# A conditioned attention block with two transformer layers: the first sequences loaded in rows, the layers' weights loaded behind the first projections, local scores in units of two heads, and a new order

## The chip, the core and the metric

The kernel runs on one core of a Trainium2 chip. Its engines work side by side: TensorE (PE) multiplies matrices and transposes, VectorE (DVE), ScalarE (ACT) and GpSimd (POOL) do the element-wise work, and SyncE (SP) as well as ScalarE issue DMAs. The metric is the device time of one execution in microseconds. All arithmetic is in 32-bit floating point.

## The reference, cut to what matters

There are 32 independent sequences of 256 tokens with 256 features. A sequence `x` and a side sequence `f` go through one conditioned attention (16 heads of 16) and two layers of local attention (8 heads of 64, windows of 128 tokens, each with the window before it) with a gated feed-forward part (hidden width 682); the result is added to `x`.

```python
# conditioned attention, for each sequence
q = (f + b_self) @ Wq + bq
k_prev, k_self = (x + b_prev) @ Wk + bk, (f + b_self) @ Wk + bk
v_prev, v_self = x @ Wv + bv, f @ Wv + bv
weights = softmax([masked(q k_prev^T), q . k_self] / 4)
h = (weights[:-1] @ v_prev + weights[-1] * v_self) @ Wo + bo
# two layers
for l in range(2):
    q, k, v = split(shift_token(h) @ wqkv[l])
    q, k = rotary(l2norm(q) * q_scale[l]), rotary(l2norm(k) * k_scale[l])
    h = h + local_attention(q, k, v) @ wo[l]
    n = layernorm(shift_token(h)) * ln_g[l] + ln_b[l]
    a, g = split(n @ w1[l] + b1[l])
    h = h + (a * gelu(g)) @ w2[l] + b2[l]
return x + h
```

## The kernel before

The kernel takes sequences in pairs (`G = 2`), so there are sixteen pairs. For each of the two sequences of a pair it runs `prepared` (load, turn, project) and `conditioned` (scores, softmax, values, output projection). Then come, for the pair, two rounds of `attention` for each sequence and `feedforward` for both together. `finished` loads `x` once more, adds, and stores. The features lie on the partitions between these steps, in one of two `stream` tensors.

None of this is issued in the order in which it is written. Every operation is first recorded in a `Plan` as part of a unit, the work that TensorE does without a break, with what the other engines do on its results. A unit has a kind: `full` uses the whole array, `rows` of 2 or 4 and `cols` of 2 or 4 divide it into tiles that work side by side. A full unit with 128 output rows that follows a `cols` unit may be run in column halves or quarters. The planner (`Plan.run`) then goes through a model of the engines and picks at each moment the ready unit with the lowest score (`policy`, line 1399). The score grows with the unit's place in the program (`AGE` times `stand`, where `stand` takes a table of shifts, `SHIFT`, with `FIRST` for the first pair and `FINAL` for the last two), with a change of tiling (`SWITCH`), with the work that the unit would heap on another engine beyond `STAY` (same tiling) or `ENTER` (new tiling), and falls with the work that it feeds (`FEED`, at most `MOST`). The other engines take what has been ready longest (`rank`, line 538). The order found is then issued from one line, so all instructions of the profile have line 567, and they are told apart by the names of their tiles. PSUM has eight banks, and SBUF tiles come from four pools (`t2`, `t4`, `e6`, `sm`); a unit starts when its tiles are free.

What the change touches:

- `load_sequence` (line 697) loads `ft` (of `f`) and `xt` (of `x`) through `blocks`, four DMAs of 64 KB each with runs of 128 bytes, on SP's queue. In this layout DVE can turn a whole tensor with one 32x32 block transpose. `prepared` (line 874) does so into `fT` and `xT`. For the first two sequences the loads are recorded before the loop.
- `prepared` projects `fT` and `xT` with `wq`, `wk` and `wv`. The tiles of the results are `cq`, `ck`, `cs` and `vals`. ScalarE adds the biases into `qc` and `kc`, and `spread` sends these with eight small SP DMAs each into `qh` and `kh`, where each head has its own partitions; `kh<-behind` adds a mask row. The unit `self` is its last.
- `conditioned` makes scores twice: `S` for the maximum (`mx`), and, once the maximum is written into `qh` (`nmT`, `rows`), `ST` for the exponentials `eT`, which `AV` weighs. `co` is the output projection.
- The weights are loaded from ScalarE's queue. `wq`, `wk`, `wv`, small vectors and constants (`misc`, whose first columns are the identity `ident`) come first, then `wo` and `bo`, and then a loop over the two layers (line 781) with `wqkv`, the rope table (`rope0`, scaled by `qks`), `wout`, `w1`, the small vectors and `w2`. Nothing holds these loads back.
- `attention` (line 1042) handles a sequence's eight heads as four pairs `c`. `scores(cs)` (line 1107) makes the scores `sc` of the pairs in `cs` in one unit of kind `rows` 2 and hands them to `weights`, which makes `ex` with DVE and ScalarE. `turned` transposes these (`exT`) and `weighed` multiplies by `v` (`av`). How many pairs make one unit is set by `CS, CX, CW = 2, 2, 2`, for the three steps in turn.

Of the kernel before, what the change touches and what calls it, by code (L numbers as in the profile page):

```python
# [19 lines left out]
P = 128  # L20
S = 256
D = 256
G = 2
# [134 lines left out]
class Plan:  # L158
# [15 lines left out]
    def __init__(self, tc, engines, pools, make):  # L174
        self.tc, self.engines, self.pools, self.make = tc, engines, pools, make
        self.nodes, self.units, self.unit_, self.group, self.place = [], [], None, 0, 0.0
        self.stage, self.stages, self.done = 0, {}, set()
# [116 lines left out]
    def run(self, policy):  # L294
# [18 lines left out]
        self.idle = self.switches = self.cold = self.wire = 0.0  # L313

# [42 lines left out]
        while todo:  # L357
# [12 lines left out]
            if e != "PE":  # L370
# [12 lines left out]
                if n.load:  # L383
                    self.wire = max(self.wire, end) + n.load
                    end = self.wire + self.LANDING
                ended(n, end)
# [151 lines left out]
    def rank(self, n, e):  # L538
        other = e == "S" and n.table not in ("any", None, self.table)
        return n.ready + 2.0 * other, n.number  # L540
# [32 lines left out]
class Engine:  # L573
# [11 lines left out]
CS, CX, CW = 2, 2, 2  # L585
# [3 lines left out]
    156, 528, 54, -76, 49, 292, -28, 245, 120, -102, -425, 52, -30, 35, 68, 22, 33, 22, -208,  # L589
    -4, 119, -41, 61, 69, 90, 152, 19, 32, -62, -238, 52, -2, 49, -168, 13, -85, -54, -65, 36,  # L590
    64, 112, -439, -349, -167, 223, -408, -5, 62, -46, -234, 56, -27, 119, -7, -45, 96, -17,
    -38, 61, -374, -335, -58, 1, -150, -372, -152, -51, -265, -409, 8, 67, -53, 114, -41, -17,
    -83, 34, 68, 48, 60, -261, -99, -7, -76, -335, -100, -105, -191, -306, -58, 15, -102, 32,
    -23, -66, 39, -309, -188, 106, -258, 33, -30, -139, 22, -141, 82, -290, -255, 32, 19, -99,
    134, 126, 14, -15, -222, -574, -156, 97, 93, -32, -241, 50, 152, -118, -41, -45, 21, -102,
    20, 47, 3, 15, 55, 169, -56, -24, 43, 199, -247, 143, -97, -15, -223, -41, -95, -88, -212,
    -127, -29, -32, -285, -545, -142, -265, -8, -118, -6, 152, 84, -122, 25, 14, 4, 18, 141, 60,
    166, -454, -139, 25, -127, -186, -20,
]
FIRST = [  # L600
    0, 0, 0, 0, 0, 0, 0, 0, 10, 35, -9, 213, 102, 95, 210, -345, -65, -122, -290, 49, -201, 6,
    -193, -61, -7, 106, 99, -6, -100, -16, 106, 13, 65, -266, -137, 7, -58, 247, 58, 69, 48, 1,
    -114, -155, -32, -173, -34, 65, 135, 130, -117, 69, 71, 117, 272, 156, 73, -3, -1, -31, -33,
    -133, 51, 151, 175, 239, 445, 215, 231, 120, 135, 97, -3, -90, -188, -357, -32, -64, -276,
    -297, -374, -330, -535, -346, -72, -135, -217, 156, 27, 182, 40, -174, -48, 77, -252, -118,
    -307, -246, 33, -96, -400, -238, -150, -69, -239, 6, 79, 152, 26, -38, -60, -358, -15, -155,
    89, -99, -69, -60, 87, -3, -114, -222, -118, 60, -143, -246, -29, -171, -319, -115, -49,
    -17, -96, -75, -88, 113, 144, -56, -6, 35, -9, -141, -41, -74, -183, -115, -131, -49, -79,
    109, -65, -145, 55, -88, -244, -157, -153, -264, -181, -118, -121, -82, -23, -37, -86, -83,
    -110, -213, -219, -209, -160, -63, 0, 0,  # L610
]
FINAL = [
    0, 0, 0, 0, 0, 0, 0, 0, 56, -34, 24, 16, 12, 140, -55, -63, -14, 1, -33, -84, -66, -53, -46,
    -145, -40, -121, 67, -19, -32, -29, 98, 97, 8, 45, -119, -130, -61, -106, 67, 94, -33, 8,
    54, 33, 8, -94, -222, -47, -210, -95, -90, -11, -121, 156, 49, 10, 43, 87, 7, 64, -144, -81,
    35, -80, 47, -31, -76, -182, 53, 86, 32, 67, 229, 49, 115, 31, 6, -10, -135, 40, 27, -79,
    -83, -8, 108, -110, 63, -40, -249, -98, -95, -18, -170, -139, -28, -12, -41, 76, 83, 116,
    59, -9, 65, -157, -74, -50, -119, -145, -16, -25, 13, 6, 73, -2, -181, -184, -151, -49, -97,
    116, -8, 56, 187, 15, 69, -31, -42, -59, 109, 161, 193, 112, 209, 211, 117, 80, 41, 59, 77,
    -84, 136, 47, 92, -54, 145, 66, 93, 1, -60, 152, -30, 108, 108, -119, 50, -9, -29, -39, 44,  # L620
    -113, -118, -128, -103, 66, 10, -89, -27, -49, -2, -10, 53, 34, -67, -8,
# [4 lines left out]
def tile_kernel(ctx: ExitStack, tc: tile.TileContext, a: dict, out: bass.AP):  # L626
# [69 lines left out]

    def load_sequence(n, after=()):
        plan.unit(after=after)
        loaded[n] = [blocks(name, src[n]) for name, src in (("ft", f), ("xt", x))]

    load_sequence(0)
    plan.unit()

# [5 lines left out]
    wq, wk, wv = (weight(f"w{n}", a[f"L0_cond_W{n}"], D) for n in "qkv")  # L709
# [10 lines left out]
    bk = column(a["L0_cond_bk"], "bk", 2)  # L720
    bv = kept("bv", (P, D))
    ld(bv, a["L0_cond_bv"].partition_broadcast(P), act)
    ld(misc, a["c_misc"][:, 0:C_IOTA], act)
# [45 lines left out]
    load_sequence(1)  # L769
# [3 lines left out]
    plan.unit()  # L773
    wo = weight("wo", a["L0_cond_Wo"], D)
    bo = column(a["L0_cond_bo"], "bo", 2)
    rope0 = sb2("rope0", P, 2, 4, FD)
    ld(rope0, a["c_rope"].rearrange("(t p) j d -> p t j d", p=P), act)
# [3 lines left out]
    for l in range(DEPTH):  # L781
# [63 lines left out]

    def projected(name, w, j, src):
# [605 lines left out]
```

## Time and profile before

| what | us |
|---|---|
| median of 3 runs (3422.1 to 3424.76) | 3423.85 |
| the profiled execution | 3422.27 |
| its span, first to last instruction | 3420.5 |
| TensorE busy | 3348.6 |
| VectorE busy | 2161.9 |
| ScalarE busy | 1780.5 |
| GpSimd busy | 1163.4 |

The profile is of one execution. A row of a timeline gives the start, the duration, the engine (with a q for the issue of a DMA), the line, the operation, the output and inputs by name, the number of instructions merged into the row, and, in brackets, the idle time before it with what ended it. A row of the stretches gives the stretch, its length, the busy time and instructions of PE, PEld (weight loads), DVE, ACT and POOL, then the granted TensorE clock as a share of full speed, the busy share of the DMA engines, and GB/s.

### The profile page before, as it was taken

The numbers are of one execution on the slowest core, as the hardware profiler recorded it, in microseconds if no ns is written. First come the engines' busy times: TensorE is split into PE (matmuls) and PEld (weight loads), VectorE is DVE, ScalarE is ACT, GpSimd is POOL, SyncE is SP. The second block draws the span as 40 slices with busy tenths as digits, with TensorE's granted clock in tenths as the row PEclk, the third lists the DMA queues.
The fourth block names the chain that finished last, engine by engine and source line by source line (L and its number), as shares of the span: only waits on it lengthen the run. The fifth ranks groups of instructions, "written<-read, shape, count | busy, mean of one in ns | idle before, by whom it ended". The sixth has DMA issues, their size and how long they took to land.

```text
span 3420.5 us, 69279 instructions
## 1 busy us (share of the span) xinstructions
PE 3348.6 (98%) x25984; PEld 1908.7 (56%) x25984; DVE 2161.9 (63%) x6673; ACT 1780.5 (52%) x4537; POOL 1163.4 (34%) x1195
## 2 busy tenths in 40 slices
PE   6999999999999999999999999999999999999998
PEld 5665556465564655656455564655646556465554
DVE  3558567485675747657485674847657486574763
ACT  0556456473554726456373563735547364554653
POOL 0325052250613407043160522507134070432541
PEclk7999999999999999999999999999999999999999
DMA  5100010010101001010010100101010010100001
GB/s 147 20 15 11 12 27 9 16 26 9 26 15 21 17 13 20 16 20 17 13 21 14 27 13 15 24 7 26 16 20 17 13 20 15 27 15 12 4 2 27
DMA packets 310926, 69.00 MB, mean 20 GB/s; under 512 B 286776, under 2 KB 308096, under 8 KB 310592
## 3 DMA queue, kind: packets, MB, share of 16 engines
q1 hardware_dynamic: 298848, 54.24, 9.3%
q10 hardware_dynamic: 11744, 10.34, 1.1%
q8 instruction: 207, 3.39, 0.4%
q14 instruction: 127, 1.04, 0.1%
HBM read 35.53 MB, written 8.39 MB: 13 GB/s over the span
## 4 chain that ended last, share of the span: by engine, by line
PE 77%; DVE 12%; POOL 3%; ACT 1%; issue 1%; POOLq 0%; SPq 0%; DMA 0%; DVEq 0%; ACTq 0%
PE w L567 27%; DVE ex L567 6%; PE wout L567 6%; PE q L567 5%; PE av L567 4%; PE k L567 4%; PE sc L567 4%; PE S L567 4%; PE v L567 3%; PE ST L567 3%; PE vals L567 3%; PE AV L567 3%; PE exT L567 2%; PE qkT L567 2%; DVE rot L567 2%; PE cs L567 2%
## 5 line engine op out<-in xcount | busy, mean ns | idle before, releaser
L567 ACT ACTIVATE ex<-ex,nm,rq 128x128 f32<-128x128 f32 (+1 forms) x1024 | 546.2, 537 | 107.3 <-DVE nm L567 106.1
L567 PE MATMUL w<-cen,w 128*128 128x512 f32 (+2 forms) x1480 | 589.2, 598 | 0.8 <-DVE cen L567 0.3
L567 POOL TENSOR_TENSOR raw<-raw,rot 128x512 f32<-128x512 f32 x256 | 327.6, 1281 | 749.2 <-DVE rot L567 660.3
L567 PEld LDWEIGHTS w<-cen,w 128*128 128x128 f32 (+2 forms) x1480 | 224.9, 175 | 270.7 <-issue 231.4
L567 DVE TENSOR_SCALAR ex<-ex,den 128x128 f32<-128x128 f32 (+1 forms) x1024 | 351.4, 457 | 5.2
L567 DVE TENSOR_REDUCE mx<-S 128x2 f32<-128x512 f32 x512 | 314.3, 686 | 49.4 <-PE S L567 49.3
L567 PE MATMUL w<-act,w 128*128 128x512 f32 (+3 forms) x880 | 324.6, 602 | 2.9 <-DVE act L567 2.8
L567 ACT ACTIVATE eT<-ST 128x512 f32<-128x512 f32 x512 | 263.8, 605 | 115.0 <-PE ST L567 109.8
L567 DVE CUSTOM_DVE_ANT_0 ex<-sc,misc 128x128 f32<-128x128 f32 (+1 forms) x1024 | 299.2, 353 | 31.3 <-PE sc L567 30.8
L567 DVE SCALAR_TENSOR_TENSOR act<-w,b,act 128x512 f32<-128x512 f32 (+1 forms) x192 | 143.4, 748 | 262.0 <-PE w L567 195.5
L567 ACT ACTIVATE act<-w,b 128x512 f32<-128x512 f32 (+1 forms) x192 | 128.9, 686 | 280.1 <-PE w L567 276.8
L567 POOL TENSOR_TENSOR xs<-stream 128x512 f32<-128x512 f32 x32 | 35.0, 1094 | 641.5 <-PE cs L567 318.1
L567 PE MATMUL wout<-qT,wout 128*64 128x256 f32 (+2 forms) x1728 | 242.8, 381 | 0.5 <-DVE nm L567 0.3
L567 PE MATMUL v<-wqkv,stream 128*128 128x512 f32 (+1 forms) x608 | 242.5, 599 | 0.0
L567 PE MATMUL k<-wqkv,stream 128*32 128x512 f32 (+2 forms) x1104 | 239.9, 593 | 0.0
L567 PE MATMUL q<-wqkv,stream 128*32 128x512 f32 (+2 forms) x960 | 237.7, 594 | 0.2 <-ACT stream L567 0.2
L567 ACT COPY exT<-exT 128x384 f32<-128x384 f32 x512 | 207.3, 498 | 54.5 <-PE exT L567 53.8
L567 PEld LDWEIGHTS w<-act,w 128*128 128x128 f32 (+3 forms) x880 | 124.8, 176 | 167.1 <-issue 151.5
L567 POOL TENSOR_TENSOR rq<-ss,minus_half 128x8 f32<-128x8 f32 x128 | 215.1, 1684 | 4.9
L567 POOL TENSOR_TENSOR ss<-ss,minus_half 128x8 f32<-128x8 f32 x128 | 213.3, 1666 | 5.7
L567 PE MATMUL sc<-kT,qT 64*128 64x128 f32 (+1 forms) x2048 | 205.7, 337 | 0.4
L567 PEld LDWEIGHTS wout<-qT,wout 128*64 128x64 f32 (+2 forms) x1728 | 161.6, 147 | 73.0 <-issue 17.6
(127 smaller groups left out, 5520.2 us busy)
## 6 DMA issues: line engine op xcount, KB each, us to landing
ft<-in_fside_BxSxS_dram SPq DMA_DIRECT2D x128, 64.0 KB
xt<-in_x_dram SPq DMA_DIRECT2D x128, 64.0 KB
qh<-qc SPq DMA_DIRECT2D x256, 32.0 KB
kh<-kc SPq DMA_DIRECT2D x256, 32.0 KB
ot<-in_x_dram SPq DMA_DIRECT2D x128, 64.0 KB
out_dram<-ot SPq DMA_DIRECT2D x128, 64.0 KB
wqkv<-in_L_ffn_wqkv_dram ACTq DMA_DIRECT2D x2, 1536.0 KB
w<-in_L_ffn_w_dram ACTq DMA_DIRECT2D x2, 1364.0 KB
```

The source lines that it names most:

```text
L567: ins = getattr(self.engines[n.engine], name)(*[real(v) for v in args], **{k: real(v) for k, v in kw.items()})
```

## The change

The diff has five parts, and what they compute stays the same.

1. The first two sequences are loaded by `rows`: one DMA for each tensor, token rows of 1 KB. `prepared` turns these with `turned_tiles`, which is four TensorE transposes into a PSUM bank and a copy by DVE or ScalarE. Later sequences keep `blocks`. The identity is loaded ahead of all weights, and the loads of sequence 1 are recorded before those of the lengths.
2. The loop over the layers becomes `load_layer(l, after)`. It is called in the loop over the pairs, in the first pair, after `prepared` of sequence 0 for layer 0 and of sequence 1 for layer 1, and its unit waits for the last unit of that `prepared`. The unscaled rope table is loaded once for each layer. `wv` follows the small vectors, and `wo` and `bo` have a unit of their own.
3. `CS` becomes 1, so that `scores` makes a unit for each pair of heads.
4. The planner's model of a DMA issue now waits until the eighth transfer back has landed, and `rank` can weigh the place in the program by `hurry`, which is set to 0.
5. The constants of the score and the three tables of shifts are new.

```diff
     def put(n):
...
                 if n.load:
-                    self.wire = max(self.wire, end) + n.load
+
+                    at = max(t, self.landed[-8]) + cost
+                    now[e] = at
+                    self.wire = max(self.wire, at) + n.load
                     end = self.wire + self.LANDING
+                    self.landed.append(end)
...
-        return n.ready + 2.0 * other, n.number
+        return n.ready + 2.0 * other + self.hurry * n.unit.stand, n.number
...
-CS, CX, CW = 2, 2, 2
+CS, CX, CW = 1, 2, 2
...
+    def rows(name, src):
+
+        t = sb2(name, P, 2, D)
+        ld(t, src.rearrange("(t p) d -> p t d", p=P))
+        return t
...
     def load_sequence(n, after=()):
         plan.unit(after=after)
-        loaded[n] = [blocks(name, src[n]) for name, src in (("ft", f), ("xt", x))]
+        shape = rows if n < G else blocks
+        loaded[n] = [shape(name, src[n]) for name, src in (("ft", f), ("xt", x))]

     load_sequence(0)
     plan.unit()
+    ld(ident, a["c_misc"][:, C_ID : C_ID + P], act)
...
-    wq, wk, wv = (weight(f"w{n}", a[f"L0_cond_W{n}"], D) for n in "qkv")
+    wq, wk = (weight(f"w{n}", a[f"L0_cond_W{n}"], D) for n in "qk")
...
+    wv = weight("wv", a["L0_cond_Wv"], D)
     bv = kept("bv", (P, D))
     ld(bv, a["L0_cond_bv"].partition_broadcast(P), act)
-    ld(misc, a["c_misc"][:, 0:C_IOTA], act)
+    ld(misc[:, P:C_IOTA], a["c_misc"][:, P:C_IOTA], act)
+    load_sequence(1)
+    plan.unit()
...
-    for l in range(DEPTH):
+
+    def load_layer(l, after):
+        plan.unit(after=after)
+        rope0 = sb2("rope0", P, 2, 4, FD)
+        ld(rope0, a["c_rope"].rearrange("(t p) j d -> p t j d", p=P), act)
         wqkv.append(weight(f"wqkv{l}", a["L0_ffn_wqkv"][l], 3 * INNER))
...
         ft, xt = loaded.pop(n)
-        plan.unit()
-        fT, xT = sb2("fT", P, 2, S), sb2("xT", P, 2, S)
-        for dst, src in ((fT, ft), (xT, xt)):
-            vec.transpose(dst.rearrange("p c t -> p (c t)"), flat(src))
+        if n < G:
+            fT, xT = turned_tiles("fT", ft), turned_tiles("xT", xt)
+            plan.unit()
+        else:
+            plan.unit()
+            fT, xT = sb2("fT", P, 2, S), sb2("xT", P, 2, S)
+            for dst, src in ((fT, ft), (xT, xt)):
+                vec.transpose(dst.rearrange("p c t -> p (c t)"), flat(src))
...
             heads.append(prepared(n, b))
+            if p == 0:
+                plan.stage = (-1, 1 + b)
+                load_layer(b, (plan.unit_,))
...
-    STRETCH, AHEAD, LAST = 2.75, 3, 14
-    AGE, SWITCH, OVER, STAY, ENTER = 0.02, 1.5, 1.0, 6.0, 4.0
+    STRETCH, AHEAD, LAST = 2.5, 3, 14
+    AGE, SWITCH, OVER, STAY, ENTER = 0.02, 0.5, 0.5, 8.0, 1.5
     HURRY = 0.0
-    FEED, MOST, BANKS = 1.0, 3.0, 0.0
+    FEED, MOST, BANKS = 1.0, 2.0, 0.5
```

## The prediction

> **What bounds the kernel now.** I read four views in this order: the page's busy rows and slices, the table of stretches, the timeline of the first 120 us, and TensorE's waits and timeline in one period of the middle. From the page:
>
> ```profile
> span 3420.5 us, 69279 instructions
> PE 3348.6 (98%) x25984; PEld 1908.7 (56%) x25984; DVE 2161.9 (63%) x6673; ACT 1780.5 (52%) x4537; POOL 1163.4 (34%) x1195
> ...
> PE   6999999999999999999999999999999999999998
> ...
> PEclk7999999999999999999999999999999999999999
> ```
>
> TensorE is busy in 98% of the span; no other engine reaches two thirds. So time can come only from TensorE: its idle time (71.9 us), its slow clock, or its own work. The first slice is the odd one: 6 tenths busy, clock 7. The stretches (PE busy, then the other engines, the granted clock, DMA share and rate) open it up:
>
> ```profile
> 0.00:10.00 10.00, 2.21 (x11) 2.24 (x11) 2.09 (x7) 0.00 (x0) 0.50 (x5) 1.00 0.79 156
> 10.00:20.00 10.00, 3.04 (x15) 2.95 (x14) 0.49 (x5) 0.00 (x0) 1.89 (x1) 1.00 1.00 249
> ...
> 40.00:50.00 10.00, 6.06 (x29) 5.97 (x28) 0.27 (x2) 0.00 (x0) 0.00 (x0) 0.50 0.77 230
> 50.00:60.00 10.00, 6.48 (x32) 4.67 (x32) 3.83 (x12) 0.00 (x0) 0.45 (x2) 0.50 0.42 93
> ...
> 80.00:90.00 10.00, 10.00 (x65) 6.83 (x58) 5.64 (x10) 1.96 (x5) 0.00 (x0) 0.50 0.01 3
> ```
>
> Over all stretches to 120 us, idle is 28.6 us. Busy time multiplied by the missing share of the clock gives another 22.9 us, and the first query projections (3.78 us, where the same eight records take 1.99 us at 65.69) 1.9 us that the clock column misses. So about 53 us are lost before 120 us. From 120 to 3400 us the same table has 31.8 us of idle at clock 1.00, and the last 20.5 us have 11.5. Why the opening is slow is in its timeline:
>
> ```profile
> 17.03 4.81 SPq L567 DMA_DIRECT2D ft<-in_fside_BxSxS_dram  x4
> ...
> 22.09 3.78 PE L567 MATMUL cq<-fT,wq 128*128 128x256 f32 x8 [9.05 <-DVE fT L567]
> ...
> 32.41 1.28 ACT L567 ACT_TABLE_LOAD   x1 [32.41 <-DMA w<-in_L_ffn_w_dram]
> ...
> 33.70 0.47 ACT L567 ACTIVATE qc<-cq,bias_q 128x256 f32<-128x256 f32 x1
> ...
> 50.60 4.55 PE L567 MATMUL S<-kh,qh 17*128 17x256 f32 x22 [4.54 <-DMA w<-in_L_ffn_w_dram]
> ...
> 62.20 0.47 ACT L567 ACTIVATE kc<-ck,bias_kp 128x256 f32<-128x256 f32 x1 [26.93 <-PE ck L567]
> ```
>
> Three delays stand in a row. First, the sequence's loads (eight DMAs of 128-byte runs) and a length load queued behind them hold fT until about 22 us. Second, `cq` is done at 25.9, yet `qc` starts at 33.70, because ScalarE's stream holds the layer-0 DMA issues ahead of it. Third, layer 1's issues (33.71 to 58.4) do the same to `kc` of sequence 1. Each queue pauses as if about eight transfers may be open: ACT's ninth issue waits at 6.94, SP's ninth at 12.47, when earlier ones land.
>
> **The change, part by part.**
>
> **Sequences 0 and 1 in rows.** Sixteen SP issues become four, with 1 KB runs instead of 128 bytes; four DVE transposes (0.69 us each) become sixteen TensorE transposes and four copies (0.69 us on DVE or 0.58 on ScalarE). Sequence 1 also no longer waits in SP's queue at 17.03. Before cq, about 1.1 MB must arrive (ft, xt, identity, wq, wk): 7 us at the 156 GB/s of the first stretch, 3 us at the 371 GB/s of 20 to 25 us, plus issue and landing. I take fT at 8.5 us (7 to 12), so cq some 13 us earlier. In the trace, four turns of `at` take 0.60 us warm. The Trainium skill, "TensorE: Matmul & The Clock Gate", Part 4, speaks against this move: a transpose isn't counted as activity and doesn't release the clock. The sum by the warm row is 4 × 0.60 = 2.4 us, by the rule 4.8 us with all of them cold. The first two sets surely run cold, so I take 3.6 us. They stand on the path, since nothing else is ready.
>
> **Layers loaded behind projections.** The ACT queue first gets identity, wq, wk, four small vectors, wv, bv, the masks, wo and bo; a layer's sixteen issues come only after the last unit of a sequence's `prepared`. So `qc` and `kc` of sequence 0 have nothing of the layers ahead: `qc` at about 14 us instead of 33.7, spreads (20 small SP DMAs, which took 35.2 to 58.7 us beside the weights) mostly ahead of or beside layer 0. I put the first S stage at 30 us where it ended at 60. What is late next is the same ScalarE block in another place. The sixteen issues of layer 0 ran from 9.1 to 33.3 and those of layer 1 from 33.7 to 58.4, 24 us each; after the change I expect some 20 to 40 and 42 to 62. Queued behind them are sequence 1's `qc` and `kc`, then the first `eT`; S, self and AV on TensorE wait for these. The first ST stage therefore moves from 85.88 to about 60, and the first q projection from 115.28 to about 88. The rope table, now read twice, adds 256 KB, about 1 us of DMA that weights cover. Opening in sum, transposes included: **-28 us**, bounds -12 and -40 (the whole 53 us cannot go: 8 us of arrival and a cold start stay).
>
> **One score unit for two heads.** The matmuls, mask additions and exponentials stay; 128 score units of sixteen records become 256 of eight. Each asks two banks instead of four. TensorE's price is in these rows (start, duration):
>
> ```profile
> 1102.49 3.19 PE L567 MATMUL sc<-kT,qT 64*128 64x128 f32 x32
> 1105.62 1.07 PE L567 MATMUL AV<-eT,vh 128*32 128x256 f32 x16
> ...
> 1157.61 1.58 PE L567 MATMUL sc<-kT,qT 64*128 64x128 f32 x16
> 1159.02 0.91 PE L567 MATMUL exT<-misc,ex 64*128 64x64 f32 x24
> ...
> 1179.25 1.58 PE L567 MATMUL sc<-kT,qT 64*128 64x128 f32 x16
> 1180.76 1.99 PE L567 MATMUL wout<-qT,wout 128*128 128x256 f32 x8
> ```
>
> From start to next start a unit takes 1.41 us when another row-tiled unit follows and 1.51 when a full one does: one change of tiling costs about 0.10 us. An added unit costs 0 where it stands beside row-tiled work and 0.20 alone: 0 to 26 us over 128 units. The skill's "TensorEngine Tiling (Array Packing)", Key Properties, says that changing mode drains the engine; read strictly, every added unit pays twice, 26 us, and the opening's gain is gone. The trace says that much score and transpose work adjoins. I take 0.07, **+9 us**. Against it, DVE is fed 4 us at a time (four mask passes, 2 × 0.29 + 2 × 0.42, reads, four scalings of 0.40 to 0.52) instead of 8, and fewer banks are held; TensorE's small waits on DVE and ScalarE after 120 us sum to about 28 us. I take a third of these, **-10 us**; bounds -20 and 0.
>
> **Order found anew.** The price lists of the planner change: a switch of tiling counts 0.5 instead of 1.5, backlog is tolerated to 8 instead of 6 when staying and to 1.5 instead of 4 when entering. This reshuffles everything with the same work. From 1000 to 1210 us I count 60 changes of tiling; at 0.10 us and sixteen pairs this is about 96 us of span. A cheaper switch invites more, a stricter entry fewer. Bounds -24 and +24 (a quarter either way); I take **0**. The end (PE from 3401.81, DVE, POOL, output DMA) has no edit of its own: 0, bounds -3 and +3.
>
> Sum against the profiled execution, 3422.27 us (3420.5 of span and 1.8 around it): 3422.3 - 28 + 9 - 10 = 3393. The median shown, 3423.85, is 1.6 above that execution, so I forecast **3395 us**.
>
> **The rivals.** *Weights and spreads collide* (0.20): layer 0 starts just as sequence 0's spreads do, and those need 20 us again as at 35 to 58. For it: DMA runs at 178 to 322 GB/s there; against: fewer bytes are left. The opening gives 12 and the middle stays: 3422.3 - 12 - 1 + 1.6 = 3411. *Tiling switches eat it* (0.14): smaller units and a switch price of a third raise changes from 60 to 90 per pair; 480 × 0.10 = 48 us on TensorE itself (the added score units are among these changes), against 28 won in the opening, with the middle's waits unchanged: 3422.3 + 48 - 28 + 1.6 = 3444. It decides from about 280 added changes, 17 per pair. For it: TensorE has no slack to hide them; against: neighbours of equal tiling cost nothing. *The two halves balance* (0.06): 3424. That the layers don't move at all is excluded only if the planner heeds the new edge; nothing it prices may bring them ahead of that unit.
>
> **How the numbers follow.** The main case has 0.60. A measurement of this kernel can tell about 0.2%, 6.8 us, from no change. Main and collision cases give faster 0.80; balance gives 0.06, switching 0.14. The range reaches from an opening of -40 and a middle of -16 (3368) to most of the switching case (3430), leaving about 0.2 out.
>
> **What would show it.** Right: PE's first slice at 8 or 9; `cq` before 10 us; `qc` before 17 without a wait for a layer's DMA; first q projection at 80 to 95; idle to 120 us under 18. PE busy after 120 us within 15 us of 3257. Wrong: S still waiting on kh spreads beyond 45 us (collision), or `sc` and the changes of tiling adding over 28 us of TensorE time after 120 (switching).

## The result, and the profile after

The kernel after takes **3460.64 us** (3458.92 to 3462.82), beside 3423.47 for the kernel before in the same comparison: a ratio of 1.0109, interval 1.0091 to 1.0126. It is 37 us slower, where 29 us less was forecast. The page of the kernel after (busy rows, TensorE's slices and clock, then the shares of the chain that ended last):

```profile
span 3457.1 us, 67916 instructions
PE 3373.3 (98%) x25400; PEld 1965.6 (57%) x25400; DVE 2184.5 (63%) x6737; ACT 1764.7 (51%) x4473; POOL 1174.6 (34%) x1195
...
PE   7999999999999999999999999999999999999998
...
PEclk7899999999999999999999999999999999999999
...
PE 63%; DVE 20%; ACT 6%; POOL 5%; issue 2%; DMA 0%; SPq 0%; POOLq 0%; DVEq 0%; ACTq 0%
```

The same chain in the kernel before:

```profile
PE 77%; DVE 12%; POOL 3%; ACT 1%; issue 1%; POOLq 0%; SPq 0%; DMA 0%; DVEq 0%; ACTq 0%
```

The shares of busy time tell nothing: TensorE is at 98% in both. The chain does. Work that leads to the end passes through DVE, ScalarE and GpSimd for 31% of the span, against 16% before.

Where the time went is seen from one marker, the first reduction `mx<-S` on DVE of each pair of sequences (the sixteen pairs are counted from 0, and the order repeats from pair to pair). Three stretches, in us; the marker stands at another place in the new order, so only the period and the total compare exactly:

| kernel | start to pair 5 | pair 5 to pair 15 | pair 15 to end | one period (mean of six) |
|---|---|---|---|---|
| before | 993.1 | 2025.1 | 402.3 | 207.3 |
| after | 993.3 | 2055.2 | 408.6 | 210.15 |
| difference | +0.2 | +30.1 | +6.3 | +2.85 |

So the gain that was forecast for the opening does not show (the first stretch also holds pairs 0 to 4; the sums to 120 us below are of the opening alone), and most of the loss is made in the repeating part: nearly 3 us in every pair.

**The opening.** TensorE's stretches (columns as before):

```profile
0.00:10.00 10.00, 4.91 (x21) 3.93 (x22) 2.88 (x6) 0.00 (x0) 0.19 (x4) 1.00 0.78 200
10.00:20.00 10.00, 10.00 (x38) 8.98 (x39) 0.87 (x7) 2.28 (x4) 2.39 (x3) 1.00 0.20 54
...
40.00:50.00 10.00, 3.33 (x16) 3.37 (x16) 1.89 (x9) 0.00 (x0) 0.45 (x2) 0.50 0.72 227
50.00:60.00 10.00, 6.84 (x31) 6.59 (x31) 0.27 (x2) 0.00 (x0) 0.00 (x0) 0.50 0.75 224
...
80.00:90.00 10.00, 10.00 (x69) 8.73 (x70) 3.89 (x9) 0.37 (x1) 0.00 (x0) 0.50 0.01 2
```

The first 20 us are much better than before, and DMA, at 100% then, now runs at 54 GB/s. The bytes come later, at 40 to 60 us, and there the hole is. To 120 us TensorE idles 24.4 us instead of 28.6, but the half clock now takes 27 us of its busy time instead of 23 (the last row above: TensorE full, at 0.50): the two cancel. The clock column has no record before 18 us, where a set of turns takes 1.1 us instead of 0.60. The timeline of TensorE and ScalarE:

```profile
4.33 1.09 PE L572 MATMUL turn<-misc,ft 128*128 128x128 f32 x4 [4.33 <-DMA ft<-in_fside_BxSxS_dram]
...
14.11 2.05 PE L572 MATMUL cq<-fT,wq 128*128 128x256 f32 x4
...
16.20 0.47 ACT L572 ACTIVATE qc<-cq,bias_q 128x256 f32<-128x256 f32 x1 [0.39 <-PE cq L572]
...
46.66 8.66 PE L572 MATMUL b<-lb,w 128*128 128x1 f32 x40 [11.15 <-DMA lb<-in_L_ffn_ln_b_dram]
...
59.34 3.81 PE L572 MATMUL S<-kh,qh 17*128 17x256 f32 x16 [3.16 <-DMA kh<-kc]
...
68.41 0.47 ACT L572 ACTIVATE kc<-ck,bias_kp 128x256 f32<-128x256 f32 x1 [40.22 <-DMA lb<-in_L_ffn_ln_b_dram]
```

and of SP's queue:

```profile
24.77 13.89 SPq L572 DMA_DIRECT2D qh<-qc  x16
38.76 13.48 SPq L572 DMA_DIRECT2D kh<-behind  x8
52.34 22.86 SPq L572 DMA_DIRECT2D kh<-kc  x16
```

`cq` starts 8 us earlier and `qc` 17.5 us earlier than before, and then all is given back: the new order issues the spreads of both sequences' `qh` first, then eight `behind` rows, and only then `kh`. The spread that the first S stage needs last is the 32nd issue; before it was the 20th. S starts at 59.34 (before 50.60). The last `kc` stands behind the layers' issues for 40 us, and the first q projection comes at 117.78 instead of 115.28.

**The score units.** The `sc` group on the page (busy, mean ns, idle before it and its releaser), after and before:

```profile
L572 PE MATMUL sc<-kT,qT 64*128 64x128 f32 (+1 forms) x2048 | 207.7, 337 | 9.0 <-ACT kT L572 5.8
```

```profile
L567 PE MATMUL sc<-kT,qT 64*128 64x128 f32 (+1 forms) x2048 | 205.7, 337 | 0.4
```

Twice the units cost 2 us of work in the new order, in which a score unit follows another at 141 places; changes of tiling, counted by the shapes of TensorE's records, fell from 1011 to 965 in the whole program. What grew is the wait in front of them.

**One period.** TensorE's waits from marker to marker, kernel after (us in total, times, longest):

```profile
PE ck L572 <- DVE xT L572: 1.2, 1, 1.2
PE sc L572 <- ACT kT L572: 0.5, 1, 0.5
PE cq L572 <- DVE fT L572: 0.4, 1, 0.4
PE qkT L572 <- POOL raw L572: 0.4, 1, 0.4
PE self L572 <- DVE prod L572: 0.3, 1, 0.3
```

and before:

```profile
PE exT L567 <- ACT sq L567: 0.5, 1, 0.5
PE turn L567 <- POOL at L567: 0.2, 1, 0.2
PE qkT L567 <- DVE rot L567: 0.2, 1, 0.2
```

From start to start of TensorE's records, a pair has 205.9 us of work and 1.4 of waits before, 207.1 and 3.0 after. The longest of these waits is for `xT` on DVE, which stands at the end of a stretch in which DVE has no gap:

```profile
1133.00:1153.00 20.00, 19.63 (x93) 11.19 (x92) 20.00 (x60) 14.56 (x46) 15.96 (x16) 1.00 0.17 27
1153.00:1173.00 20.00, 18.69 (x154) 11.58 (x155) 14.55 (x39) 11.88 (x31) 14.94 (x15) 1.00 0.11 23
```

DVE is busy 20.00 of 20 us (in fact for 40.2 us, from 1125.1 to 1165.3; the longest such run in a period of before is 20.5 us), and TensorE's worst row follows.

### The profile page after: what moved, and what is told of

It reads as the page before. It is cut to its first block, busy times and chain, and to the rows that moved or that the text cites. A ratio compares the mean times of both kernels' runs of the same rounds, so it can differ in the third digit from the quotient of the medians.

```text
span 3457.1 us, 67916 instructions
## 1 busy us (share of the span) xinstructions
PE 3373.3 (98%) x25400; PEld 1965.6 (57%) x25400; DVE 2184.5 (63%) x6737; ACT 1764.7 (51%) x4473; POOL 1174.6 (34%) x1195
## 4 chain that ended last, share of the span: by engine, by line
PE 63%; DVE 20%; ACT 6%; POOL 5%; issue 2%; DMA 0%; SPq 0%; POOLq 0%; DVEq 0%; ACTq 0%
PE w L572 27%; DVE ex L572 9%; PE wout L572 5%; PE S L572 4%; ACT ex L572 4%; PE av L572 4%; PE ST L572 3%; POOL raw L572 3%; PE AV L572 2%; PE vals L572 2%; PE k L572 2%; PE v L572 2%; PE q L572 2%; PE exT L572 2%; DVE rot L572 2%; DVE raw L572 2%
## 5 line engine op out<-in xcount | busy, mean ns | idle before, releaser
L572 PE MATMUL w<-act,w 128*128 128x512 f32 (+2 forms) x780 | 326.2, 605 | 0.0
L572 PEld LDWEIGHTS w<-act,w 128*128 128x128 f32 (+2 forms) x780 | 127.0, 187 | 165.0 <-issue 158.7
```

Source lines behind the costliest of these rows:

```text
L572: ins = getattr(self.engines[n.engine], name)(*[real(v) for v in args], **{k: real(v) for k, v in kw.items()})
```

## Experiments

In all of them the planner's list of units is kept as it is in the kernel named, and then edited by a function `moved(order)`; no order is found anew. `earlier(order, preds, n, stop)` moves a unit or instruction up to the first place that its inputs and its buffers allow. Each ratio is to the kernel before, which took 3424.4 to 3425.8 us in these comparisons.

One thing has to be taken out before the periods of these runs are compared. In six periods of before and of after (pairs 5 to 10) the clock is granted in full. In after_dve, after_halves, after_full, after_ex_halves and after_best some periods hold a stretch of 3.41 us (in after_full up to 6.83) at half clock. Two neighbouring periods of after_dve and two of after_best:

```profile
995.90:1206.10 210.20, 206.81 (x1570) 120.82 (x1569) 137.05 (x421) 109.49 (x279) 73.14 (x74) 1.00 0.10 18
1206.10:1417.90 211.80, 208.36 (x1570) 121.91 (x1569) 137.20 (x422) 109.57 (x279) 73.18 (x74) 0.99 0.10 17
```

```profile
1195.40:1402.50 207.10, 205.14 (x1900) 105.13 (x1898) 133.61 (x414) 113.03 (x287) 73.14 (x74) 1.00 0.10 18
1402.50:1611.10 208.60, 206.62 (x1900) 105.82 (x1898) 133.67 (x413) 112.85 (x287) 73.23 (x74) 0.99 0.10 18
```

The same instructions take TensorE 1.5 us longer. What brings the clock down in one period and not in the next, no run shows; in after_dve it falls within 1 us after a wait of 2.1 us, in after_best some 2 us after one of 0.6. "Undisturbed" below means a period without such a stretch.

### The opening: queues

**after_pool**: the layers' loads on GpSimd's queue.

```diff
+    loads = [n for n in order if n.engine == "S" and n.load and n.unit.stage in ((-1, 1), (-1, 2))]
+    kept = [n for n in loads if not n.tiles]
...
+    for n in kept:
...
+        n.engine = "G"
+        stop = earlier(order, preds, n, stop) + 1
```

> The kernel after, its order kept, but the layers' weights (except the rope table and the q and k scales) are issued from GpSimd's queue right after the first loads, so that they move while the DMA engines stand at 0 to 69 GB/s (15 to 30 us) and ScalarE has nothing to hold it from 27.8 to 68.4 us. Theory 'the delayed loads eat the opening's gain': kc of sequence 1 at about 28 us instead of 68.4, the first q projection before 100 us instead of 117.8, the kernel 15 to 22 us faster than the kernel after. Rival 'weights and spreads collide whatever the queue': the spreads of qh and kh still end after 60 us, gain under 6 us.

Measured 3455.59 us, 1.0092 (1.0075 to 1.0110): 5 us better than after. The loads now start at 1.3 us and compete with what is needed first: `cq` moves from 14.1 to 21.6, and the `kh` spreads still end at 63, as the rival said.

**after_pool2** and **before_pool2**: only the twelve large loads go there (in the kernel after behind GpSimd's copy into `kh`, so from 14 us).

```diff
+    big = sorted((n for n in order if is_weight(n)), key=lambda n: n.number)
...
+    stop = copied[0] + 1
+    for n in big:
...
+        n.engine = "G"
+        stop = earlier(order, preds, n, stop) + 1
```

> The kernel after, its order kept, but the twelve large weight loads are issued from GpSimd's queue after its copy into kh (about 13 us), layer 0 first, the small ones stay on ScalarE's. The first try (all loads from GpSimd at 1 us) put cq back from 14.1 to 21.6 us and won 5 us. Theory 'the delayed loads eat the opening's gain': cq stays at 14 us, the weights move from 13 to 45 us, kc of sequence 1 is done at 32, first q projection at 95 to 105 us instead of 117.8, 12 to 20 us faster than the kernel after. Rival 'the spreads collide with the transfers in any order': under 6 us.

> The kernel before, its order kept, but the twelve large weight loads of the layers are issued from GpSimd's queue after its copy into kh (about 12 us) instead of ScalarE's. Theory 'the opening is held by ScalarE's blocked queue': qc starts at 24 us instead of 33.7 and kc of sequence 1 is not held to 62; the first q projection comes 10 to 20 us sooner, about 3410 us, faster than both kernels. Rival 'the spreads and the transfers set it': the kh spreads still end near 58 us, within 5 us of the kernel before.

after_pool2: 3456.32 us, 1.0091 (1.0076 to 1.0106). SP's spreads in it:

```profile
24.87 25.88 SPq L572 DMA_DIRECT2D qh<-qc  x16
```

The same sixteen spreads took 13.89 us above; beside 330 to 386 GB/s of weights they take 25.88, and S starts at 58.65. before_pool2: 3439.43 us, 1.0043 (1.0028 to 1.0058). There the loads went out at 1.3 us, and the eight loads of the first sequence in 128-byte runs were issued on SP only by 35.8 us (in before by 12.4):

```profile
40.81 3.78 PE L567 MATMUL cq<-fT,wq 128*128 128x256 f32 x8 [16.45 <-DVE fT L567]
```

Another queue takes a load out of a sequencer's way, not out of the way of other transfers. The Trainium skill, "DMA: Bandwidth & Descriptors", Issuing engines are not separate DMA queues, says so too, and adds that concurrent issue saves only sequencer time; the two rows bear it out and put a price on it.

**after_kc**: all `qc` and `kc` and all spreads ahead of the layers' issues, the first S unit with them, the `b1` units behind the first q projection. **before_kc**: each layer's loads behind `kc` of its sequence, `b1` late.

```diff
+    for n in early:
+        if order.index(n) > stop:
+            stop = max(stop, earlier(order, preds, n, stop) + 1)
+    return bias_late(order)
```

> The order of after is kept, with three things moved in the opening: all qc and kc evictions and all qh/kh spreads of both sequences go ahead of the 32 layer loads in ScalarE's and SP's streams, the first S unit goes up with them, and the two b1 units go behind the first q projection on TensorE. If what ate the opening's gain is that spreads run beside the weights and that kc of sequence 1 and b stand behind the layers' issues: first S at about 45 us instead of 59, first q projection at 100 to 106 instead of 118, and 10 to 16 us off the time, 3445 to 3451. If the opening's loss is the cold clock and the amount of work, and the waits only fill it: first q within 3 us of 118 and the time within 4 us of 3460. The period of 210 us per pair stays in both.

> The order of before is kept, with the same idea: each layer's 16 loads stand behind kc of its sequence in ScalarE's stream, and the two b1 units go behind the first projections; sequences are still loaded in blocks and score units are whole. If the blocks of layer issues ahead of qc and kc are what makes before's opening slow: qc starts at about 26 instead of 33.7, S at 45 to 50 instead of 50.6 to 60, first q projection at 101 to 107 instead of 115, and 8 to 14 us off 3425: 3411 to 3417, which would beat both kernels. If weights behind the projections only move the collision, as the comparison of the two traces says for after: within 4 us of 3425. The period of 207.2 us stays in both.

Both theories missed: 3475.50 us, 1.0150 (1.0135 to 1.0165) and 3449.64 us, 1.0072 (1.0057 to 1.0087), 15 and 25 us slower than their parents. Nearly all of it is in the first stretch (1008.3 and 1014.4 us), the period is the parents'. In after_kc the S stage starts at 53.56, no more than 6 us earlier: even with every `kc` done by 32 us the 32nd of SP's issues sets it. The first q projection comes at 114.41 instead of 117.78. The loss stands behind it: the `b1` units, which ran at half clock in idle time, now stand in the path from 119.03 to 134.97 (5.1 and 1.0 us for one layer, 8.7 and 1.0 for the other), at half clock from 123.0 on. In before_kc S does start at 40.89 instead of 50.60, but then `cq` of sequence 1 waits 9.76 us for `mx` on DVE, the first q projection comes at 114.90 (before 115.28), and `b1` fills 126.47 to 144.30. So these two runs mix two moves: the place of the loads was worth 3.4 and 0.4 us to the first q projection, and the place of `b1` cost 16 to 18. No run moved the loads and left `b1`.

**after_spq**: SP's spreads in the order of need (sequence 0 first), layer 0's loads behind `kc`, layer 1's weights on SP behind the rows, each `b1` later.

```diff
+    spreads.sort(key=lambda n: (n.unit.stage, "b" not in name_in(n), n.number))
...
+    order = behind(order, preds, set(loads[0] + small), last)
+    order = behind(order, preds, set(weights), rows)
+    for n in weights:
+        n.engine = "D"
```

> The order of after is kept, but the opening's queues are put in the order in which they are needed: SP spreads sequence 0 first (behind, qh, kh), then sequence 1; the layer loads stand behind kc of both sequences in ScalarE's stream, with the weights of layer 1 moved to SP behind the rows of both sequences; each layer's b1 unit stands where a bank comes free later. Theory (spreads): S waited until 59 because its last spread was the 32nd of 40 issues on SP, at 0.9 to 1.7 us each. Eight qc spreads from 25 us and eight kh spreads at 0.62 each put the first S at 36 to 40, the first q projection at 95 to 108, and the time at 3440 to 3452. Rival (the knot): with S early, the next in-order queue (DVE's rope products that wait for a layer's loads, or ScalarE's issues) takes the wait and b1 loses its idle time: first S early, but first q within 6 us of 118 and the time at 3456 or more.

The rival was right: 3473.87 us, 1.0148 (1.0131 to 1.0165). S starts 13 us earlier than in after, the first q projection comes no earlier (118.08, after 117.78), and the start to pair 5 takes 7 us longer; some 5 of these are `b1` of layer 1, which now runs behind that projection, from 135.47. TensorE, DVE and GpSimd in it:

```profile
45.99 8.54 PE L572 MATMUL S<-kh,qh 17*128 17x256 f32 x50 [10.93 <-DMA kh<-kc]
63.51 3.26 PE L572 MATMUL S<-kh,qh 17*128 17x256 f32 x14 [8.98 <-DVE mx L572]
```

```profile
62.09 0.77 DVE L572 TENSOR_TENSOR rope<-rope,qks 128x64 f32<-128x64 f32 x6 [7.66 <-DMA qks<-in_L_ffn_k_scale_dram]
```

```profile
109.02 0.45 POOL L572 COPY w1t<-w 128x84 f32<-128x84 f32 x2 [21.98 <-DMA lg<-in_L_ffn_ln_g_dram]
...
110.69 1.48 PE L572 MATMUL turn<-misc,at 128*128 128x128 f32 x4 [10.62 <-POOL at L572]
```

`mx` is ready to run but stands behind a rope product that waits for a layer's scales; `at` stands behind GpSimd's copy that waits for layer 1's weights. With SP's order mended, DVE's and GpSimd's in-order streams hold TensorE instead. So the order of the spreads did delay S, but S alone was not what the opening was short of: SP has 32 issues up to the one that S needs, and ScalarE's, DVE's and GpSimd's in-order streams each have something that waits for a layer's DMA ahead of a sequence's work.

### Score units and column halves

**before_split**: each score unit of before in two, the second half behind the next unit on TensorE (1011 changes of tiling become 1047).

```diff
+            held = Node("PE", None, n.number)
+            held.ops, held.soft, held.tiling, held.parent = n.ops[4:], False, n.tiling, n
+            n.ops = n.ops[:4]
```

> The kernel before, its order kept, but each score unit of two pairs of heads is cut into two and the second half is issued after the next unit of TensorE (where no reader forbids it). This adds 36 changes of tiling (1011 to 1047 in the whole program). Theory 'a half unit costs little': 36 changes at 0.10 us and somewhat later masks, 2 to 10 us slower than the kernel before. Rival 'every unit pays its own drain' (the switching case of the prediction): 128 times 0.20, 26 us slower or more, which would explain most of the loss.

3437.76 us, 1.0041 (1.0027 to 1.0054): 12 us, 1.0 us in each period: +0.57 per pair as waits of `ck` on DVE, +0.45 as TensorE's own time. That is about the size that the prediction gave the split by itself, but it had counted changes of tiling alone.

**before_full** and **after_full**: nothing in column halves or quarters.

```diff
+        if n.engine == "PE" and n.soft and n.ops:
+            n.tiling = ("full", 1)
```

> The kernel before, its order kept, but no full unit is run in column halves or quarters any more. Before, 700 us of TensorE's time went in column halves after 120 us, in the kernel after 411 us. Theory 'the new order loses the column halves': they save time on the narrow outputs (var, self) and on the weight loads of v, k and q; without any the kernel before is 15 to 30 us slower, and the kernel after has lost some 40% of that. Rival 'halves cost and save nothing': within 5 us of the kernel before.

> The kernel after, its order kept, without any column halves or quarters. Leaving them out of the kernel before cost it 37 us (3462.6 against 3425.5). Theory 'the new order uses the halves less': after 120 us the kernel after spends 411 us in halves where the kernel before spends 697 us, so leaving them out costs about 37 x 411 / 697 = 22 us, 3483 us, and some 15 us of the change's loss is this. Rival 'both orders gain the same by halves': 37 us again, 3498 us, and the halves explain nothing of the loss.

3462.56 us, 1.0115 (1.0097 to 1.0134), and 3491.71 us, 1.0199 (1.0165 to 1.0232): 37 us for before. For after the size is unclear: its four executions spread from 3480.82 us at a mean clock of 0.989 to 3508.23 at 0.982. The first is 20 us over after, which had 0.989 too. Undisturbed periods say the same: 211.8 us in after_full, 1.6 more than after, where before_full has 3.2 more than before. So the halves are worth about 1% to before and some 0.6% to the new order, near the 22 us of the first theory. They pay at the matmuls with 1 or 8 output columns: var +0.84 and self +0.80 us per pair in before_full. The new order has fewer: 411 us of TensorE's time in halves after 120 us, where before has 697.

**after_halves** and **before_halves**: the opposite, each unit that can run in halves does.

```diff
+        if n.engine == "PE" and n.soft and n.ops and n.tiling == ("full", 1):
+            n.tiling = ("cols", 2)
```

> The order of after is kept, but every matmul unit that could run in column halves and runs whole in after does run in halves (TensorE time in column halves after 120 us is 411 us in after, 697 in before). If the column halves that the new order has lost are worth their time (var and self with outputs of 1 and 8 columns cost 0.84 and 0.80 us per pair more when before runs them whole): var and self fall by at least 0.9 us per pair and the time by 10 to 20 us, 3440 to 3450. If halves only pay where a neighbour is in halves already, since each further change of tiling costs about 0.1 us, or because twice the instructions cost as much: within 5 us of 3460 or slower.

> The order of before is kept, and every soft matmul unit that ran whole in it runs in column halves. Before waits only 1.4 us per pair and its period is TensorE's own work, so if each half of a small matmul saves what the ledger says (0.37 us per pair for var and 0.37 for self in after), it could fall by up to 6 us, to 3418, and beat both kernels; but before has most of these in halves already (697 us of 3257), and added changes of tiling at transposes (0.1 us each, exT and vals +0.4 and +0.5 per pair in after) may cost as much: within 5 us of 3425.

3449.71 us, 1.0070 (1.0053 to 1.0086), and 3423.18 us, 0.9998 (0.9989 to 1.0008). In after, 11 us come back, but not where expected: the profile has -5.0 us before pair 5, -2.3 at the end, and none in between. There two things eat the gain. In an undisturbed period (209.3 us, 0.8 less than after) TensorE's work is 1.3 us less (var and self -0.37 each; `exT` +0.4) and its waits are 0.56 us more. And most periods hold a stretch at half clock, which gives 1.5 us back, at `vals` and `rs`. That 0.56 of 1.3 us comes back as waits says that TensorE alone does not set the period any more. In before nothing is won: changes of tiling rise from 1011 to 1163, TensorE's work rises by 0.7 us per pair and its waits fall by 0.5.

### What sets the period

**after_dve**: the transposes into `fT` and `xT`, for which `cq` and `ck` wait, up to eight DVE instructions earlier. **after_act**: the copies `oh`, `aT` and `av` from DVE to ScalarE.

```diff
+        while i > 0 and k < EARLY:
+            i -= 1
+            k += order[i].engine == "V"
+        earlier(order, preds, n, i)
```

```diff
+        if n.engine == "V" and hasattr(n, "either") and n.ops[0][1][0].tile.name in ("oh", "aT"):
+            n.engine = "S"
+        elif n.engine == "V" and hasattr(n, "either") and n.ops[0][1][1].tile.name == "av":
+            n.engine = "S"
```

> The kernel after, its order kept, but each transposition of fT and xT stands eight VectorE instructions earlier in VectorE's stream (less where its load or its buffer forbids it). Theory 'waits of the new order': TensorE stands 1.24 us in front of ck and 0.4 us in front of cq in nearly every pair because VectorE reaches xT and fT late; these waits (13.8 and 5.6 us in sum) go, and the kernel is 12 to 20 us faster than the kernel after. Rival 'VectorE is full there': what is pushed back (the normalisations of ex) makes TensorE wait instead; within 4 us of the kernel after.

> The kernel after, its order kept, but the copies of oh, of aT and of the result of av that the planner gave VectorE (128 copies, 0.42 to 0.69 us each) are done by ScalarE. Theory 'VectorE is too full in the stretch before ck' (busy without a gap for 40 us in each pair, and moving the transpositions earlier made it worse by 12 us): these 4 us per pair come off VectorE and the waits of ck, cq and self (1.9 us per pair) mostly go, 10 to 25 us faster than the kernel after. Rival 'ScalarE's stream then holds TensorE instead': within 5 us of it or slower.

3472.56 us, 1.0144 (1.0123 to 1.0165): 12 us slower. The wait of `ck` grew from 1.23 to 2.10 us per pair, but the undisturbed period is that of after (210.2 us, the rows above): what is lost is a stretch at half clock in each of the six periods from pair 6 on. And 3464.05 us, 1.0118 (1.0101 to 1.0135): no gain, though DVE has 3.7 us less per pair. Neither an earlier place for the two instructions nor less DVE work somewhere in the period is what is missing.

**after_ck**: the v projection behind `ck` goes ahead of it.

```diff
+        for n in [n for n in order[i:] if named(n)][1:7]:
+            if named(n) == "v" and earlier(order, preds, n, i) == i:
+                break
```

> The order of after is kept, but in every pair the v projection behind the first ck and cq of the second sequence goes ahead of that ck, which waits 1.23 us for xT on DVE in each period. If the waits of after's order are local (a unit asked for a little too early), the wait goes and the period falls by about 1.2 us: 13 to 17 us off the time, 3444 to 3447. If TensorE and DVE are in step and each wait only says that the chain through DVE is the longer one, the wait appears again at a later unit: within 4 us of 3460.

3461.17 us, 1.0107 (1.0091 to 1.0122): no change. Its waits in one period begin with

```profile
PE exT L572 <- ACT qc L572: 1.1, 1, 1.1
```

The wait of `ck` is gone and 1.1 us stand in front of `exT` a few units on. The place of `ck` in TensorE's order is not the cause; TensorE stands as long a few units later for what DVE and ScalarE deliver.

**after_ex**: in each pair the eight scalings `ex<-ex,den` inside DVE's gapless run, between the first `fT` and the last `xT`, go to ScalarE.

```diff
+        for n in order[min(turns, default=0) : max(turns, default=0)]:
+            if n.engine == "V" and n.ops[0][0] == "tensor_scalar" and named(n) == named(n, 1) == "ex":
+                n.engine = "S"
+                n.ops = [
+                    ("activation", (args[0], args[1], AF.Identity), {"scale": args[2]})
+                    for name, args, kw in n.ops
+                ]
```

> The order of after is kept, but in every pair the eight scalings of ex by 1/den that stand on DVE between the first fT and the last xT of the next pair (two groups, about 3.8 us) are done by ScalarE in the same place. Theory (DVE's run without a gap): from 1125 to 1165 us DVE has no gap, and TensorE's waits behind it (ck for xT 1.23 us, then exT) are its lateness: DVE ends 3.8 us earlier, ck's wait goes and does not come back elsewhere, the period falls from 210.1 to 208.5 to 209.0, the time by 14 to 22 us. Rival (order alone): the wait is in the order and returns at another unit, or ScalarE becomes late in DVE's place: period within 0.4 of 210.1 and the time within 5 us of 3460.

3454.98 us, 1.0090 (1.0075 to 1.0105). The period is 208.3 us, 1.8 less, so the first theory holds there; `ck`'s wait is gone and appears nowhere else. DVE's run without a gap is 31.6 us instead of 40.2; it ends in the second of these rows (DVE was busy 14.55 of 20 in the row shown above for after):

```profile
1129.00:1149.00 20.00, 19.61 (x93) 11.17 (x92) 20.00 (x60) 14.54 (x46) 15.95 (x16) 1.00 0.17 27
1149.00:1169.00 20.00, 20.00 (x177) 12.99 (x177) 11.18 (x31) 15.70 (x40) 14.93 (x15) 1.00 0.15 30
```

The total fell by 6 us only, because the rule also caught 32 scalings, not eight, in the last pair: pair 15 to the end took 417.2 us instead of 408.6.

**after_ex_halves**: both edits. **after_best**: both, the scalings only in pairs 2 to 14 and only those of layer 1 of the pair two back (the edit against that of after_ex).

```diff
-    for p in range(1, T // G):
+    for p in range(2, 15):
...
+            if n.unit.stage == (p - 2, 7, 1) and n.engine == "V" and n.ops[0][0] == "tensor_scalar" and named(n) == named(n, 1) == "ex":
```

> Both edits at once: the eight scalings per pair on ScalarE, and every soft matmul unit that ran whole in column halves. In after, halves took 0.30 us per pair of TensorE's work and gave 0.56 back as waits. If DVE's run is what ate it, then with DVE relieved the work saved counts: the period is another 0.3 us below that of the scalings alone. If not, halves add nothing to the scalings here either (but for some 5 us in the opening).

> As the run with scalings on ScalarE and with column halves, but the scalings are moved only where the order repeats (pairs 2 to 14, eight each); in the last two pairs the earlier kernels had also moved others, and their end from the first S of the last pair was 413 to 417 us instead of 408.6. If the repeating order alone gives the gain: the periods stay at 208.2 on average, the end comes back to 406 to 409, and the time is 3432 to 3439. It would still be 8 to 14 us behind before, as the period is 1 us longer and the fill of the first pairs some 5 us.

3442.08 us, 1.0053 (1.0038 to 1.0068), and **3429.00 us, 1.0010 (1.0001 to 1.0020)**: of the 37 us that the change costs, eight scalings per pair on another engine and the column halves bring back 32. after_best did better than expected: start to pair 5 986.7 us, to pair 15 2037.9, to the end 406.1. Against after that is -6.6, -17.3 and -2.5. On average the halves add 0.15 us per period to the scalings (208.3 to 208.2), less than the 0.3 expected; in undisturbed periods they add 1.2 (to 207.1, where before has 207.2), and half clock in two of three periods takes that back. No version here beats the kernel before.

**before_ex**: the same eight scalings in the order of before.

> The order of before is kept, and the same eight scalings per pair (layer 1 of the pair two back, in pairs 4 to 14) go to ScalarE. If DVE's gapless run is what binds after and not before, where DVE has gaps of 1.3 to 2.6 us that end on ScalarE's squares: the period stays within 0.3 us of 207.2 and the time within 4 us of 3425. If DVE is late in both kernels: the period falls by 0.5 us or more and the time by 6 us or more, and this version beats both.

3463.64 us, 1.0108 (1.0089 to 1.0127): neither theory. The edit that gains in after costs 39 us here, 3.3 us per period. Its two largest waits in a period, then the stretch in before_ex, and the one that answers to it in before (ScalarE is the number ahead of (x64) in both):

```profile
PE sc L567 <- DVE qT L567: 1.1, 1, 1.1
PE qkT L567 <- ACT qT L567: 1.0, 1, 1.0
```

```profile
1163.00:1183.00 20.00, 17.69 (x202) 12.33 (x202) 12.63 (x66) 19.13 (x64) 1.40 (x2) 1.00 0.01 2
```

```profile
1153.00:1173.00 20.00, 20.00 (x219) 14.73 (x218) 17.61 (x80) 18.62 (x64) 1.98 (x2) 1.00 0.02 5
```

In before these scalings fall where ScalarE is already busy 18.6 of 20 us. Eight more (about 0.5 us each) do not fit: the copies `qT` and `kT` behind them are late, and TensorE stands for 2.3 us in this stretch. So the long run of DVE without a gap belongs to the new order, and before has a ScalarE that is nearly full there instead. The relief is a property of the place, not of the operation.

## Why the prediction was wrong, by its steps

- **Opening, -28 us: failed, measured +0.2 to pair 5.** The early part came nearly as told: turns at 4.33, `qc` at 16.20 (before 17 was named). `cq` did not start before 10 but at 14.11, since the four sets of turns and the three `bias` sets, all cold, stand ahead of it; the 5.0 us of `bias` were in no term of the sum. The turns took 4.4 us, close to the 4.8 that the skill's rule gave and not the 3.6 taken; as the `bias` sets, which are no transposes, ran cold too, this agrees with the rule and does not prove it. The step that failed is "spreads mostly ahead of or beside layer 0", with S at 30. Twenty spreads were counted; SP has forty in the new order, thirty-two of them up to the last that S needs, at 0.87 us each and up to 1.7 beside the weights. The sign of the collision (S beyond 45) came true, and the 12 us that this rival still gave the opening were too kind. S alone is not the whole step: with S forward by 13 us (after_spq) the first q projection came no earlier, as `mx` and `at` then waited for layers' loads. First q at 117.78, 24.4 us of idle and a first slice of 7 fail the marks of 80 to 95, 18, and 8 or 9. No run took the rows or the later loads of the change alone, so what each is worth stays open.
- **Score split, +9: the size about right, in part by luck.** before_split cost 12 us, but over half of that is a wait of `ck` that this step did not count. In the new order the split shows as 2 us of `sc` and 9 us of waits ahead of it.
- **The middle's waits, -10: failed, wrong in sign.** Waits per pair rose from 1.4 to 3.0 us, about 16 us over the repeating pairs. The step took it that DVE, fed in smaller pieces, would be less late. Instead the new order packs score masks, scalings, rope products and transposes into one run of 40 us without a gap. The trace of before could not show this run; what it did show is a DVE at 63% with 18.55 of 20 us in its fullest stretch and a run of 20.5 us without a gap, and a share of the span was read as slack. after_ex is the proof by experiment: eight scalings less in that run, and the period is 1.8 us shorter.
- **Order, 0: failed.** The bounds of ±24 held changes of tiling alone. These fell by 5%, and column halves became fewer: var and self cost 0.92 us more per pair. The rest of the 1.2 us of added work is moves of both signs (S +0.8, v and `av` +0.3 each, `w` -0.7, `qkT` -0.5); no run separates them. TensorE's busy time after 120 us grew by 20 us, where within 15 was the mark.
- **End, 0: +6.3.** Only in after_halves and after_best is a part of it back (2.3 and 2.5); the rest was not tried.
- **The rival on the other side, 3444, had the right sign for a wrong reason**: changes of tiling fell instead of rising to 90 per pair.

What stays open: after_best is still at 1.0010 of before. Its mean period is 0.9 us longer, all of it in stretches at half clock; its one execution with a mean clock of 0.987 took 3422.90 us, where before took 3428.17 to 3429.27 with 0.988. What sets the clock in these periods was not tested. And the opening of 28 us less may exist in some order of all four streams at once; no run found it.

## What to carry to other kernels

Where an engine is full, ask of any other engine whether it has a stretch without a gap in the period, rather than what its share of the span is; the wait behind such a stretch moves when the waiting unit is moved, and goes only when the stretch is shortened. A load that is taken out of one in-order stream is found again in the next: list every stream (SP, ScalarE, DVE, GpSimd) that has something waiting for it before costing the move, and count the issues ahead of the one that is awaited. An edit that relieves one order can cost another as much: before reusing it, look at the receiving engine in that very stretch. And read the granted clock of every period before a difference of 1 or 2 us in it is explained by waits.

## What the runs showed of the hardware

- Four scalings of `ex` on DVE took 1.15 us or nearly twice that, within one period of the kernel after:

```profile
1129.87 1.15 DVE L572 TENSOR_SCALAR ex<-ex,den 128x128 f32<-128x128 f32 x4
...
1158.03 2.17 DVE L572 TENSOR_SCALAR ex<-ex,den 128x128 f32<-128x128 f32 x4
...
1158.63 1.29 POOL L572 TENSOR_TENSOR raw<-raw,rot 128x512 f32<-128x512 f32 x1
```

  GpSimd was idle during the first. In the second the excess is in the last of the four, which began at 1158.70, took 1.50 us and ended 0.28 us after GpSimd's product. Of the 1024 scalings in this trace, the 705 that met no work of GpSimd took at most 0.52 us each, the others up to 1.53. The Trainium skill, "Advanced Engine Details and Errata", VectorE Performance Modes, notes that VectorE's second port to SBUF is shared with GpSimd, so that the two block each other when VectorE uses both; these rows agree, and no run here took GpSimd's part away to prove it.
- A spread's issue on SP took 0.63 to 0.66 us with few other transfers, 0.87 in the opening of after, 1.7 there for the `behind` rows beside 227 GB/s (13.48 us for 8), and 1.6 beside 330 to 386 GB/s (25.88 us for 16).
- Sixteen var matmuls per pair, with one output column each, take 1.79 us from start to start when whole (before_full), and 0.98 us as thirty-two column halves (after_halves): 0.11 us for each product against 0.06, though twice as many instructions give the same outputs.
